# Finding where each node's run begins in a sorted edge list: marks multiplied with the list's differences instead of 49 gathers of rows

## The chip, the core and the metric

The kernel runs on one core of one Trainium2 chip. A core has a matrix engine (TensorE, PE in the profile), three elementwise engines (VectorE or DVE, ScalarE or ACT, GpSimd or POOL), a queue engine (SyncE, SP) and 16 DMA engines that all the queues share. Each engine works through its own list of instructions in order and waits for others by semaphores. The metric is the device time of one execution in microseconds. The kernel before takes 6495.99 us in the median of 5 runs (6495.36 to 6511.66).

## The reference, cut to what matters

The program is two layers of a graph network over 6250 nodes with 256 features. Each layer has a message-passing part, a linear attention part and a feed-forward part with experts. The last part of the second layer is a graph attention (GAT) that decides how the experts are weighted:

```python
src = jnp.concatenate([edge_index[0], loops])
dst = jnp.concatenate([edge_index[1], loops])
e = jax.nn.leaky_relu(a_src[src] + a_dst[dst], negative_slope=0.2)
e_max = jax.ops.segment_max(e, dst, num_segments=M)
ee = jnp.exp(e - e_max[dst])
denom = jax.ops.segment_sum(ee, dst, num_segments=M)
...
agg = jax.ops.segment_sum(msg, dst, num_segments=M)
```

The edge list has 131,072 random edges. The kernel sorts them by destination once. The sums and maxima over the edges of one node are then running scans over a stretch of the list, and for each node the kernel must know the place in the list where its stretch begins (`gfirst`) and where it ends (`glast`). The work in question computes those two tables of places.

## The kernel before, in words

**The sorted list.** `by_gat` is a table in DRAM of 128 runs of 1024 keys (128x1024 int32, 512 KB). A key holds the destination node in its upper bits and the source in its lower 13. Read row by row it is the list in order of the destination. It is finished long before it is used here.

**The places before (`gat_places`, line 701 on).** The place of node n is the number of keys smaller than n's least key. Nodes stand in 49 tiles of 128, one node a partition. First the 128 first keys of the runs are turned into a row by TensorE (lines 712 to 716), and for each of the 49 tiles one VectorE instruction counts how many of them are smaller (line 720): that gives the run that holds the node's first edge. Then, for each tile, an indirect DMA on POOL's queue fetches that run for each of the 128 nodes (the tile `grow`, 128x1024 f32, 512 KB; helper `gather`, line 770), and one VectorE instruction counts the smaller keys in it (line 734). The gather of tile t is issued two turns ahead of its count. The end of the function writes the places to DRAM and reads them back shifted by one node (lines 741 to 745), because the end of a stretch is the beginning of the next one.

**Where this runs.** `middle` (line 1535) sets up three pieces of work that share the engines. The main line is `experts` (line 1356): 32 slots of 512 rows, each slot with four column blocks, each block with two steps: the first products into a PSUM bank `ph` (line 1414) with a Gelu on ACT, and the second products of the slot before into `po` (line 1422) with a bias added by VectorE (line 1424). `turn` transposes the next slot's rows (line 1397). The weights and rows of a slot, 512 KB each, and its biases `mb` come over SP's queue. After the experts come `take_back`, which is 98 gathers, and `mix1`.

The second piece is `edge_sums`, which goes through 782 tiles of 128 edges: per tile one gather on POOL's queue (`ring<-in_edge_attr,edge_of`), one mark on VectorE (line 616), one product on TensorE (line 603), and per four tiles one addition on VectorE (line 594). It has 793 rounds; a gather is issued 11 rounds ahead of its product, into a ring of 15 buffers, so POOL can be at most a few rounds ahead of TensorE.

The third piece is `others`: `gat_places`, then `node_terms`, which fetches and adds rows per node with 98 gathers.

**What sets the order.** Everything is put into the queues in an order that is worked out when the program is built, from estimated costs. Each generator yields a cost for what it has just issued. `beside` lets `others` have 0.7 units for each unit of `edge_sums` (1.27 units a round); `step(3.8)` after each step of the experts lets that mixture issue 3.8 units, and `step(11)` does so 30 times in `mix1`. What is left when `mix1` is through is issued by `finish`. So a piece of `others` with smaller costs ends after fewer steps of the experts, and the rounds of `edge_sums` move with it. In this stretch there are 4 PSUM buffers named `mm`, given out in turn to `ph`, `po`, the transposes and everything else that asks for one, and 2 named `es` for the edge products.

Of the kernel before, what the change touches and what calls it, by code (L numbers as in the profile page):

```python
# [7 lines left out]
BF16 = mybir.dt.bfloat16  # L8
F32 = mybir.dt.float32
I32 = mybir.dt.int32  # L10
AF = mybir.ActivationFunctionType
OP = mybir.AluOpType
# [6 lines left out]
P = 128  # L19
N = 6250  # L20
NT = 49
# [6 lines left out]
W2C = E2 // P  # L28
# [8 lines left out]
NODE_BITS, NODE_ONE = 13, 1 << 26  # L37
# [20 lines left out]
NP_MASK = 8191  # L58


class Net:
# [639 lines left out]
    def gat_places(self, sp):  # L701

        nc = self.nc
        self.gfirst = self.const.tile([P, NT], I32, name="gfirst")
        self.glast = self.const.tile([P, NT], I32, name="glast")
        places = self.dram.tile([NP + 1, 1], F32, name="places")
        least = sp.tile([P, NT], F32, name="least")
        li = least.bitcast(I32)
        nc.gpsimd.iota(li, pattern=[[P, NT]], base=0, channel_multiplier=1)
        nc.vector.tensor_scalar(li, li, NODE_BITS, NODE_ONE, op0=OP.logical_shift_left, op1=OP.bitwise_or)  # L710
        heads = sp.tile([P, 1], F32, name="heads")
        nc.sync.dma_start(heads.bitcast(I32), self.by_gat[:, 0:1])
        ph = self.tr()
        nc.tensor.transpose(ph[:, 0:P], heads.to_broadcast([P, P]), self.ident)
        hrow = sp.tile([P, P], F32, name="hrow")
        nc.vector.tensor_copy(hrow, ph[:, 0:P])
        runs = sp.tile([P, NT], F32, name="gruns")
        junk = sp.tile([P, W2C], BF16, name="gjunk")
        for t in range(NT):
            nc.vector.tensor_scalar(junk[:, 0:P], hrow, least[:, t:t + 1], None, op0=OP.is_lt, op1=OP.add,  # L720
                                    accum_out=runs[:, t:t + 1])
            yield 0.4
        nc.vector.tensor_scalar(runs, runs, -1.0, 0.0, op0=OP.add, op1=OP.max)
        run = sp.tile([P, NT], I32, name="grun")
        nc.vector.tensor_copy(run, runs)
        inside = sp.tile([P, NT], F32, name="ginside")
        late = []
        for t in range(NT + 2):
            if t < NT:
                r = sp.tile([P, W2C], F32, name="grow", bufs=3)  # L730
                self.gather(r.bitcast(I32), self.by_gat, run[:, t:t + 1])
                late.append(r)
            if t >= 2:
                nc.vector.tensor_scalar(junk, late[t - 2], least[:, t - 2:t - 1], None, op0=OP.is_lt, op1=OP.add,
                                        accum_out=inside[:, t - 2:t - 1])
            yield 1.7
        first = runs
        nc.vector.scalar_tensor_tensor(first, runs, float(W2C), inside, op0=OP.mult, op1=OP.add)
        total = sp.tile([1, 1], F32, name="gtotal")
        nc.vector.memset(total, float(E2))  # L740
        nc.sync.dma_start(places[0:NP, :].rearrange("(t p) o -> p (t o)", p=P), first)
        nc.sync.dma_start(places[NP:NP + 1, :], total)
        end = sp.tile([P, NT], F32, name="gend")
        nc.sync.dma_start(end, places[1:NP + 1, :].rearrange("(t p) o -> p (t o)", p=P))

        none = inside
        nc.vector.tensor_tensor(none, first, end, op=OP.is_equal)
        past = sp.tile([P, 1], F32, name="gpast")
        nc.vector.tensor_scalar(past, self.lane, LAST - 0.5, None, op0=OP.is_gt)
        nc.vector.tensor_tensor(none[:, NT - 1:NT], none[:, NT - 1:NT], past, op=OP.max)  # L750
        nc.vector.tensor_scalar(none, none, float(OUT_OF_LIST), None, op0=OP.mult)
        nc.vector.tensor_add(self.gfirst, first, none)
        nc.vector.scalar_tensor_tensor(self.glast, end, -1.0, none, op0=OP.add, op1=OP.add)
        yield 1.0
# [1391 lines left out]
```

## Time and profile before

| what | value |
| --- | --- |
| median of 5 runs | 6495.99 us |
| the profiled execution: its own time, its span | 6506.26 us, 6504.4 us |
| mean granted TensorE clock | 0.730 |
| busy over the span: PE, DVE, ACT, POOL | 56%, 45%, 13%, 56% |
| `grow` gathers: 49, 947 ns median | 3094.4 to 3307.1 us (starts) |
| counts of line 734: 49, 1272 ns median | 3101.0 to 3319.1 us (starts) |
| `ring` gathers of `edge_sums`: 782 | 3027.8 to 4650.9 us (starts) |

Times in the trace are counted from the start of the span. "Busy" is the time in which an engine has an instruction at work, so a busy share far below one means waiting, and "idle before" names what ended the waiting. A float32 product of a 128x128 tile stands in the trace as two matmul records, one for each of its two passes. The granted clock is 1.0 or 0.5 at any moment; means over a stretch lie between.

### The profile page before, as it was taken

The numbers are of one execution on the slowest core, as the hardware profiler recorded it, in microseconds if no ns is written. First come the engines' busy times: TensorE is split into PE (matmuls) and PEld (weight loads), VectorE is DVE, ScalarE is ACT, GpSimd is POOL, SyncE is SP. The second block draws the span as 40 slices with busy tenths as digits, with TensorE's granted clock in tenths as the row PEclk, the third lists the DMA queues.
The fourth block names the chain that finished last, engine by engine and source line by source line (L and its number), as shares of the span: only waits on it lengthen the run. The fifth ranks groups of instructions, "written<-read, shape, count | busy, mean of one in ns | idle before, by whom it ended". The sixth has DMA issues, their size and how long they took to land. (4 is left out here: it accounts for less than half of the span.)

```text
span 6504.4 us, 55745 instructions
## 1 busy us (share of the span) xinstructions
PE 3630.3 (56%) x16292; PEld 2738.1 (42%) x16292; DVE 2898.2 (45%) x7864; ACT 871.3 (13%) x2058; POOL 3629.8 (56%) x4400
## 2 busy tenths in 40 slices
PE   5666655465656665364656677144653665555660
PEld 4555555445555554243434445033541333333340
DVE  5775555356666765563424443442420111111136
ACT  3650000040000000051111221010110111111120
POOL 1667777605656676225646566666457655555602
PEclk8787666687888867565878888567775776777675
DMA  5333323312222223123664443311231111111134
GB/s 182 91 110 102 88 85 87 94 55 84 86 84 84 86 86 88 49 71 118 210 132 142 134 137 119 86 50 47 73 90 15 34 40 33 36 37 36 37 102 148
DMA packets 382778, 563.72 MB, mean 87 GB/s; under 512 B 124687, under 2 KB 270278, under 8 KB 382286
## 3 DMA queue, kind: packets, MB, share of 16 engines
q0 software_dynamic: 150864, 331.19, 19.1%
q1 hardware_dynamic: 207812, 209.55, 10.3%
q10 hardware_dynamic: 23756, 18.97, 0.9%
q8 instruction: 143, 2.34, 0.1%
q14 instruction: 203, 1.66, 0.1%
HBM read 446.11 MB, written 113.72 MB: 86 GB/s over the span
## 5 line engine op out<-in xcount | busy, mean ns | idle before, releaser
L770 POOL DMA_INDIRECT ring<-table,src_of x1564 | 1597.9, 1022 | 1065.2 <-issue 333.6
L603 PE MATMUL es<-hot,ring 128*128 128x128 f32 x7820 | 1493.3, 347 | 1177.1 <-issue 476.4
L603 PEld LDWEIGHTS es<-hot,ring 128*128 128x128 f32 x7820 | 1314.8, 249 | 1419.4 <-issue 626.6
L770 POOL DMA_INDIRECT G<-gtab,glist x800 | 759.6, 949 | 440.4 <-DVE msg L1871 216.5
L770 POOL DMA_INDIRECT ring<-in_edge_attr,edge_of x782 | 746.2, 954 | 460.7 <-issue 183.1
L2064 PE MATMUL mm<-lw,lhT 128*128 128x256 f32 x1568 | 483.1, 428 | 534.9 <-issue 291.7
L618 DVE TENSOR_SCALAR hot<-numbers,node_of,w_of 128x128 f32<-128x128 f32 x1564 | 588.1, 402 | 217.4 <-remote 97.2
L2066 DVE TENSOR_TENSOR ly<-mm,lb 128x256 f32<-128x256 f32 x196 | 80.9, 422 | 1265.6 <-remote 773.9
L2064 PEld LDWEIGHTS mm<-lw,lhT 128*128 128x128 f32 x1568 | 326.5, 212 | 742.0 <-issue 453.1
L2056 PE MATMUL mm<-lxt,lw 128*128 128x512 f32 (+1 forms) x832 | 452.7, 663 | 64.8 <-issue 61.8
L1469 PE MATMUL mm<-ohot,ones 128*1 128x128 bf16 (+1 forms) x1564 | 152.3, 255 | 332.9 <-DVE ohot L1463 304.9
L594 DVE TENSOR_TENSOR BT<-BT,es 128x256 f32 x392 | 162.1, 414 | 375.8 <-remote 214.5
L1422 PE MATMUL mm<-mw,BT 128*128 128x256 f32 x1024 | 279.4, 419 | 63.1 <-DVE nv_node_vec_n L1498 27.5
L1414 PE MATMUL mm<-BT,mw 128*128 128x512 f32 x512 | 282.6, 677 | 55.5 <-issue 32.8
L2058 ACT ACTIVATE lhT<-mm,lb 128x512 f32<-128x512 f32 (+1 forms) x208 | 135.8, 663 | 1256.7 <-remote 876.1
L2056 PEld LDWEIGHTS mm<-lxt,lw 128*128 128x128 f32 x832 | 176.8, 219 | 234.4 <-issue 223.3
L1469 PEld LDWEIGHTS <-ones 128*1 128x1 bf16 (+1 forms) x1564 | 116.2, 105 | 365.8 <-issue 203.5
L616 DVE TENSOR_SCALAR hot<-numbers,from_of 128x128 f32<-128x128 f32 x782 | 241.0, 344 | 36.9 <-PE es L603 10.9
L1422 PEld LDWEIGHTS mm<-mw,BT 128*128 128x128 f32 x1024 | 208.4, 215 | 93.6 <-DVE nv_node_vec_n L1498 28.3
L1301 POOL DMA_INDIRECT chosen<-z,pos x98 | 99.3, 1013 | 262.7 <-DVE chosen L1224 206.1
L243 ACT COPY sx<-back 128x512 f32<-128x512 f32 x28 | 15.0, 589 | 1576.0 <-DMA ring<-table,src_of 979.4
L1474 DVE TENSOR_TENSOR deg<-deg,mm 1x128 f32 x392 | 108.8, 277 | 261.3 <-remote 102.4
(527 smaller groups left out, 4584.4 us busy)
## 6 DMA issues: line engine op xcount, KB each, us to landing
mw<-in_L_ffn_W SPq DMA_DIRECT2D x64, 512.0 KB
ring<-table,src_of POOLq DMA_INDIRECT x1564
ye<-ly SPq DMA_DIRECT2D x48, 512.0 KB
yes<-ye SPq DMA_DIRECT2D x48, 512.0 KB
xs<-chosen SPq DMA_DIRECT2D x32, 512.0 KB
yielded<-BT SPq DMA_DIRECT2D x32, 512.0 KB
G<-gtab,glist POOLq DMA_INDIRECT x800
ring<-in_edge_attr,edge_of POOLq DMA_INDIRECT x782
```

The lines of the kernel that those rows point to most:

```text
L594: nc.vector.tensor_tensor(dst, dst, ps[:, 0:h * P].rearrange("p (j n) -> p j n", j=h), op=OP.add)
L603: nc.tensor.matmul(ps[:, j * P:(j + 1) * P], lhsT=rows[:, j * P:(j + 1) * P], rhs=hot, start=(first and j == 0), stop=(last and j == h - 1))
L616: self.nc.vector.tensor_scalar(dst, self.numbers, node, None, op0=OP.is_equal)
L618: self.nc.vector.tensor_scalar(dst, self.numbers, node, w, op0=OP.is_equal, op1=OP.mult)
L770: self.nc.gpsimd.indirect_dma_start(out=dst, out_offset=None, in_=table, in_offset=bass.IndirectOffsetOnAxis(ap=idx, axis=0))
L1414: nc.tensor.matmul(ph, lhsT=w1s[s][:, j, c * P:(c + 1) * P], rhs=xTs[s % 2][:, j, :], start=(j == 0), stop=(j == 1))
L1422: nc.tensor.matmul(po[:, :C], lhsT=hTs[(s - 1) % 2][:, i, c * P:(c + 1) * P], rhs=w[:, i, :], start=(i == 0), stop=(i == 3))
L1469: nc.tensor.matmul(ps[0:row + 1, i // GE * P:(i // GE + 1) * P], lhsT=self.ones16[:, 0:row + 1], rhs=hot[:, i, :], start=(i % GE == 0), st ...
L1474: nc.vector.tensor_tensor(d, d, ps[row:row + 1, i * P:(i + 1) * P], op=OP.add)
L2056: nc.tensor.matmul(ph[:, :n * P], lhsT=w1[:, e, j, c * P:(c + 1) * P], rhs=xt[:, j, :n * P], start=(j == 0), stop=(j == 1))
L2058: nc.scalar.activation(hT[:, c, :n * P], ph[:, :n * P], AF.Gelu, bias=b1[:, e, c:c + 1])
L2064: nc.tensor.matmul(po[:, :C], lhsT=h0[:, i, c * P:(c + 1) * P], rhs=w2[:, e0, i, :], start=(i == 0), stop=(i == 3))
```

## The change

The places are computed without gathering runs. All of `by_gat` is brought on chip once as `node` (128x1024, one run a partition), and once more shifted down by one run as `prior`, whose first row is zero. The keys are cut to their destination node and turned into float32, and `node` becomes the difference between each run and the run before it. For a tile of nodes a matrix of marks is 1 where run r begins with a node smaller than the partition's node (run 0 always counts). The product of those marks with the differences adds up the differences of runs 0 to r, which is run r itself: TensorE so picks, for each node, the run that holds its first edge. It needs two products of 128x128 with 128x512 for the 1024 columns, and a third with a column of ones that counts the marks, which is the number of the run. VectorE counts the smaller nodes in the two halves straight from PSUM. The 49 gathers, the transposed heads and the 49 counts over the heads are gone. The end of the function (places to DRAM and back) stays. The costs that the function yields are 8, 3 and 2 units ahead of the loop and 0.2 and 1.4 a tile, where it was 0.4 and 1.7 a tile with two turns more.

```diff
-        least = sp.tile([P, NT], F32, name="least")
...
-        nc.sync.dma_start(heads.bitcast(I32), self.by_gat[:, 0:1])
-        ph = self.tr()
-        nc.tensor.transpose(ph[:, 0:P], heads.to_broadcast([P, P]), self.ident)
-        hrow = sp.tile([P, P], F32, name="hrow")
-        nc.vector.tensor_copy(hrow, ph[:, 0:P])
+        node = sp.tile([P, W2C], F32, name="gnode")
+        prior = sp.tile([P, W2C], F32, name="gprior")
+        nc.sync.dma_start(node.bitcast(I32), self.by_gat)
+        nc.vector.memset(prior[0:1, :], 0.0)
+        for a, n in ((0, 112), (112, 15)):
+            nc.sync.dma_start(prior.bitcast(I32)[a + 1:a + 1 + n, :], self.by_gat[a:a + n, :])
+        yield 8.0
+        for v in (node, prior):
+            vi = v.bitcast(I32)
+            nc.vector.tensor_scalar(vi, vi, NODE_BITS, NP_MASK, op0=OP.logical_shift_right, op1=OP.bitwise_and)
+            nc.vector.tensor_copy(v, vi)
+        nc.vector.memset(prior[0:1, :], 0.0)
+        yield 3.0
+        head = sp.tile([P, 1], F32, name="heads")
+        nc.vector.tensor_copy(head, node[:, 0:1])
+        nc.vector.memset(head[0:1, :], -1.0)
+        nc.vector.tensor_tensor(node, node, prior, op=OP.subtract)
+        ids = sp.tile([P, NT], F32, name="gids")
+        nc.vector.tensor_scalar(ids, self.iota[:, 0:NT], float(P), self.lane, op0=OP.mult, op1=OP.add)
         runs = sp.tile([P, NT], F32, name="gruns")
-        junk = sp.tile([P, W2C], BF16, name="gjunk")
+        inside = sp.tile([P, 2, NT], F32, name="ginside")
+        junk = sp.tile([P, 512], BF16, name="gjunk")
+        yield 2.0
         for t in range(NT):
-            nc.vector.tensor_scalar(junk[:, 0:P], hrow, least[:, t:t + 1], None, op0=OP.is_lt, op1=OP.add,
-                                    accum_out=runs[:, t:t + 1])
-            yield 0.4
+            hot = sp.tile([P, P], F32, name="gbelow", bufs=2)
+            nc.vector.tensor_scalar(hot, self.iota, float(t * P), head, op0=OP.add, op1=OP.is_gt)
+            yield 0.2
+            pr = [self.mm() for _ in range(2)]
+            for i in range(2):
+                nc.tensor.matmul(pr[i], lhsT=hot, rhs=node[:, i * 512:(i + 1) * 512], start=True, stop=True)
+            pc = self.mm()
+            nc.tensor.matmul(pc[:, 0:1], lhsT=hot, rhs=self.ones[:, 0:1], start=True, stop=True)
+            for i in range(2):
+                nc.vector.tensor_scalar(junk, pr[i], ids[:, t:t + 1], None, op0=OP.is_lt, op1=OP.add,
+                                        accum_out=inside[:, i, t:t + 1])
+            nc.vector.tensor_copy(runs[:, t:t + 1], pc[:, 0:1])
+            yield 1.4
         nc.vector.tensor_scalar(runs, runs, -1.0, 0.0, op0=OP.add, op1=OP.max)
-        for t in range(NT + 2):
-            if t < NT:
-                r = sp.tile([P, W2C], F32, name="grow", bufs=3)
-                self.gather(r.bitcast(I32), self.by_gat, run[:, t:t + 1])
-                late.append(r)
-            if t >= 2:
-                nc.vector.tensor_scalar(junk, late[t - 2], least[:, t - 2:t - 1], None, op0=OP.is_lt, op1=OP.add,
-                                        accum_out=inside[:, t - 2:t - 1])
-            yield 1.7
+        nc.vector.tensor_add(inside[:, 0, :], inside[:, 0, :], inside[:, 1, :])
+        inside = inside[:, 0, :]
```

More of the change, by code (lines that the diff above doesn't have):

```diff
@@ L706, in gat_places @@
         places = self.dram.tile([NP + 1, 1], F32, name="places")
-        least = sp.tile([P, NT], F32, name="least")
[L708 to L711, printed above, removed]
-        nc.sync.dma_start(heads.bitcast(I32), self.by_gat[:, 0:1])
-        ph = self.tr()
-        nc.tensor.transpose(ph[:, 0:P], heads.to_broadcast([P, P]), self.ident)
@@ L719, in gat_places @@
+        junk = sp.tile([P, 512], BF16, name="gjunk")
+        yield 2.0
         for t in range(NT):
-            nc.vector.tensor_scalar(junk[:, 0:P], hrow, least[:, t:t + 1], None, op0=OP.is_lt, op1=OP.add,
-                                    accum_out=runs[:, t:t + 1])
-            yield 0.4
-        nc.vector.tensor_scalar(runs, runs, -1.0, 0.0, op0=OP.add, op1=OP.max)
-        run = sp.tile([P, NT], I32, name="grun")
-        nc.vector.tensor_copy(run, runs)
-        inside = sp.tile([P, NT], F32, name="ginside")
@@ L727, in gat_places @@
-        late = []
-        for t in range(NT + 2):
-            if t < NT:
-                r = sp.tile([P, W2C], F32, name="grow", bufs=3)
-                self.gather(r.bitcast(I32), self.by_gat, run[:, t:t + 1])
-                late.append(r)
-            if t >= 2:
-                nc.vector.tensor_scalar(junk, late[t - 2], least[:, t - 2:t - 1], None, op0=OP.is_lt, op1=OP.add,
-                                        accum_out=inside[:, t - 2:t - 1])
-            yield 1.7
+            hot = sp.tile([P, P], F32, name="gbelow", bufs=2)
```

## The prediction

> **What bounds the stretch now.** I read first the table of windows over the stages in which the pieces share the engines. Its columns: stretch, length, busy time and count of PE, PE's weight loads, DVE, ACT and POOL, granted clock, DMA share, GB/s. The rows: the count of heads; the 49 gathers; the wait at the end of the places; `node_terms`; experts beside `edge_sums` alone; a stretch without such gathers.
>
> ```profile
> 3064.00:3093.00 29.00, 28.90 (x113) 18.88 (x114) 22.82 (x124) 11.23 (x15) 7.55 (x8) 0.90 0.37 114
> 3093.00:3322.00 229.00, 156.76 (x591) 109.56 (x590) 101.32 (x251) 29.05 (x42) 140.85 (x149) 0.81 0.62 209
> 3322.00:3354.00 32.00, 5.35 (x16) 2.70 (x15) 0.98 (x7) 0.00 (x0) 2.01 (x3) 0.66 0.83 8
> 3354.00:3971.00 617.00, 429.81 (x1700) 299.85 (x1700) 263.93 (x790) 119.17 (x220) 372.82 (x386) 0.87 0.46 139
> 3971.00:4077.00 106.00, 76.79 (x328) 58.10 (x328) 30.26 (x112) 11.27 (x15) 69.58 (x74) 0.82 0.29 81
> 4661.00:4757.00 96.00, 94.67 (x544) 85.23 (x544) 69.87 (x233) 39.47 (x81) 33.64 (x34) 0.96 0.39 124
> ```
>
> Count POOL's gathers: 149 in 229 us, 386 in 617, 74 in 106. That is one per 1.43 to 1.60 us whatever the mixture. So POOL's gathers set the pace there, though POOL is busy for only 0.60 to 0.66 of the time. The groups of the second row show what fills the pace:
>
> ```profile
> L770 POOL DMA_INDIRECT ring<-in_edge_attr,edge_of x100 | 94.6, 946 | 40.2 <-issue 26.6 <-remote 9.6 <-PE es L603 2.4
> L734 DVE TENSOR_SCALAR_CACHE_REDUCE gjunk<-grow,least 128x1024 bf16<-128x1024 f32 x49 | 62.4, 1273 | 16.1 <-DMA grow<-by_gat,grun 9.8 <-issue 6.0 <-DVE hot L616 0.2
> L770 POOL DMA_INDIRECT grow<-by_gat,grun x49 | 46.4, 946 | 51.1 <-DVE gjunk L734 34.5 <-issue 11.2 <-DVE grun L725 4.6
> ```
>
> A gather is 0.95 us and 0.30 us of issue: 1.25 us unhindered, 1.5 with the waits. Last, TensorE's order in time, for its prices:
>
> ```profile
> 3079.95 1.88 PE L1414 MATMUL mm<-BT,mw 128*128 128x512 f32 x4
> 3081.67 0.38 PE L603 MATMUL es<-hot,ring 128*128 128x128 f32 x2
> 3081.89 1.89 PE L1422 MATMUL mm<-mw,BT 128*128 128x256 f32 x8
> 3083.62 0.61 PE L603 MATMUL es<-hot,ring 128*128 128x128 f32 x4
> 3084.07 0.60 PE L1397 MATMUL mm<-ident,xs 128*128 128x128 f32 x4
> 3084.50 1.88 PE L1414 MATMUL mm<-BT,mw 128*128 128x512 f32 x4
> ```
>
> Differences of the starts, at the full clock: a step of the experts 1.72 us (so 0.43 for one pass over 512 columns), one round of edges 0.22, a transpose group 0.43.
>
> **What goes.** 49 `grow` gathers: 49 x 1.25 = 61 us of POOL, 74 at 1.5; 25.7 MB of the 47.95 MB that the DMA moved there. On DVE 49 x (1.273 + 0.083) = 66 us, and 49 counts of heads at 0.342 + 0.083 = 21 us. On PE the transposed heads; it waited for their load until 3064.09, though `xs` was issued five microseconds earlier (3054.42). I take 3 us for that; bounds are 0, if the weights are as late, and 5. A POOL iota of 0.19 us, a VectorE shift and two conversions of 0.2 go at no gain, beside idle time.
>
> **What comes, by engine.**
> DMA and SP: three loads of `by_gat`, 1 MB, in place of the one of the heads, issued at about 3059.5 behind the first slot's rows and weights and ahead of the second slot's. At the 209 GB/s of the row above 1 MB is 5 us. They land near 3069, and VectorE asks for them only after the fourth step, about then; if they are later, the edge marks and the additions of `po` stand behind that wait on VectorE, and TensorE behind those. The second slot's weights, issued at 3067, slip by up to 5 us; the 3 us from the heads cover them. The sum takes 0 for both together; the bounds are -5 and +5. The memset that the shifted load may wait for runs on an idle VectorE.
> DVE ahead of the loop: two shifts, two conversions, one subtraction of 128x1024. The rows at 128x800 are 0.572 us (shift), 0.570 (conversion) and 0.984 (two inputs), so about 0.72, 0.72 and 1.25 by length: 4.1 us once. DVE is idle for 128 of the 229 us.
> DVE a tile: the mark, between 0.22 (from 0.569 for 128x800 of plain one-input work) and 0.345 (line 616, from PSUM); two counts over 512 from PSUM, between 0.69 (a 128x512 copy from PSUM) and 1.27 (the whole 1024), I take 0.77 plus 0.083; a one-column copy, 0.15. Together some 2.2 us, against 1.36 + 0.43 before: 49 x 0.4 = 20 us more, in idle time as a sum; where it stands in the order is another matter (below).
> PE a tile: two products over 512 columns in two passes each, 4 x 0.43 = 1.72 us, and the counting product, two passes with the marks loaded again. No row has one column; with 24 columns (line 169, 160 records in 18.6 us) a pass is 0.116, so 0.23; bounds 0.05 and 0.8. Together 1.95 us, 49 x 1.95 = 96 us.
>
> **What moves.** The costs yielded fall from 107.3 to 92.4 units, and `edge_sums` gets 1/0.7 of that. Before, 107.3 + 107.3/0.7 = 261 units, less 6 of the first `step`, at 3.8 a step: 67 steps of the experts stand ahead of the end of the places; after, 92.4 + 132 = 224 units make 57. Followed through the loops, the first order has 20 transpose groups and 108 edge products there (the end comes behind the last `ph` of slot 8), the second 17 and 91 (behind the third `ph` of slot 7). `node_terms` and its rounds are unchanged behind it; ten steps move to where the experts run beside edges alone; 12 rounds of edges move out of `finish`.
>
> **The sum.** PE ahead of the end of the places, before: 67 x 1.72 + 20 x 0.43 + 108 x 0.22 = 148 us of the 258 between 3064 and 3322. After: 57 x 1.72 + 17 x 0.43 + 91 x 0.22 + 96 = 221 us. POOL has 91 x 1.25 to 1.5 = 114 to 137 us there, so TensorE becomes the bound. What can it do in practice? Where it was the bound beside edges (3064 to 3093: 12 steps, 6 groups, 12 products, 25.9 us) it took 29 us: 89%. So 248 us. To that come waits that the order makes. The mark of a tile is issued behind the addition of `po` on DVE in 27 of the 49 cases, and the tile's products follow directly. TensorE then waits for its own second products to be added (0.42), for two marks of edges (2 x 0.26) and for the tile's mark (0.22 to 0.345), less the edge products between: about 1.0 us, 27 us in all (bounds: 0, if the marks are early; 49 x 1.0). T = 275 us. The end of the places comes at 3061 + 275 = 3336 where it was 3322: +14. Its wait of 32 us for the places read back remains: VectorE stands, PE behind it, POOL behind PE, SP's next loads behind the readback. Then the ten steps that were not done: 106 us for 25 steps is 4.2 each, +42. At the end 12 rounds fewer: between 8 (20 us for 31 rounds from 4641 on) and 15 (12 x 1.25), I take -12, nearer the gathers since the last 11 rounds have none. The sum is +44, less 2 for transfers that no longer meet 512 KB gathers: **+42 us**. The profiled execution's 6506.3 becomes 6548; it lies 10 us above the median, so for the median 6496 + 42 = 6538 us.
>
> **Two rules of the Trainium skill.** The granted clock was 0.81 among the gathers and 0.90 where PE was dense beside edges. "TensorE: Matmul & The Clock Gate" (Part 1, The HAM clock gate) says that only an idle window of about 3.4 us halves the clock. By it waits of 1.0 us leave the clock alone and T stays 275; by the row of 0.81 T would be 334. Against the change speaks "SBUF — State Buffer" (the "DVE blocks DMA" trap): a VectorE instruction in a two-port mode, SBUF to SBUF, keeps POOL from writing the descriptors of its DMAs. The edge marks read PSUM, the new ones SBUF. By the rule POOL loses up to 49 x 0.345 = 17 us; by the rows POOL has over 100 us to spare there, and the sum stays.
>
> **The rivals.** With the other terms kept, the change is T - 233 us.
> *TensorE takes the places in its idle time* (faster). Place: the loop. For it: 110 us of PE's 258 are without work, and the halved DMA load could shorten the waits for weights. T = 221; 3 us more at the end (15 rounds' worth for 12), and the 10 us by which PE waits for `mb` behind the places, which 3 steps in place of 1 could cover: 221 - 233 - 3 - 10 = -25, 6471. Without those 13 us it is a clear gain only below T = 220. Against: no stretch beside edge gathers ran above 89%.
> *The change gives back what it takes* (no change). T between 220 and 246, the marks always early: 6483 to 6509. For it: 22 of the 49 marks stand behind a first product, whose 1.72 us hide them.
> *Buffers and clock* (much slower). Each tile takes three of the four `mm` buffers in turn, so the experts' next product waits for the tile's counts; gaps then keep the clock at 0.81: 221/0.81 = 273, over 0.89 = 307, + 27 = 334, so +101: 6597. For it: PE was held at 0.81 for 229 us. Against: there it waited for POOL, and longer products fill its gaps.
>
> **How the numbers follow.** A measurement here tells about 0.2%, 13 us. Chances: faster 0.12, no change 0.15, the sum (+13 to +70, 6509 to 6566) 0.50, much slower 0.23. So slower by over 0.2% has 0.73. Range 6487 to 6590, which cuts most of the faster case and the far end of the last.
>
> **What would show it.** Right: 49 x 6 new matmul records between 3080 and 3335 at 0.43 us a pass, PE over 85% busy there with POOL waiting for PE's `es`, the loop's waits on PE released by the new marks; the readback's wait at about 3336; the experts' end some 55 us later than 4077; a shorter stretch behind `mix1`. Wrong: PE under 75% busy with a buffer or VectorE as releaser and the clock near 0.8 (worse than the sum), the readback's wait ahead of 3295 (better), or a node load that lands after 3080 and holds VectorE.

## The result, and the profile after

The kernel after takes 6519.48 us in the median of 27 runs (6498.76 to 6536.15), beside 6499.58 us in 50 runs of the kernel before on the same chip: a ratio of 1.0031, 95% interval 1.0023 to 1.0038. It is slower by 20 us (15 to 25). 6538 was predicted, +42.

The experiments further down ran on three other chips. There the same kernel before takes 5441.4 to 5443.1 us, and the change costs more: 5486.9 against 5442.4 us, a ratio of 1.0085 (1.0068 to 1.0102), +44.5 us. That is within the 20 to 45 us expected before it ran there; the rival, that the 20 us of the first chip came from stalls that only that chip has, is out. The loop of the kernel before had been expected to take 250 to 270 us on any chip, since its waits are for its own gathers; it took 210 (below). So each experiment is compared by its ratio to the kernel before on its own chip, and its profile with profiles of the kernels before and after taken on such a chip.

The table of windows of the kernel after, on the first chip, for the stretches that answer those shown of before. The columns are the same: stretch, length, busy time and count of PE, weight loads, DVE, ACT and POOL, granted clock, DMA share, GB/s. The rows: the loop of the places; the wait at its end; `node_terms`; experts beside edges alone; the last edge rounds at the end of `finish`.

```profile
3071.00:3305.00 234.00, 214.03 (x831) 131.78 (x830) 126.75 (x434) 27.98 (x39) 84.63 (x90) 1.00 0.27 83
3305.00:3337.00 32.00, 8.65 (x36) 5.84 (x34) 1.27 (x11) 1.47 (x2) 1.54 (x2) 0.68 0.77 12
3337.00:3958.00 621.00, 438.11 (x1706) 305.69 (x1707) 267.41 (x803) 118.26 (x218) 374.75 (x388) 0.85 0.45 136
3958.00:4108.00 150.00, 102.02 (x441) 76.94 (x439) 38.13 (x140) 16.57 (x23) 96.21 (x102) 0.83 0.32 95
...
4665.00:4676.00 11.00, 6.80 (x38) 5.63 (x36) 4.05 (x13) 0.00 (x0) 0.00 (x0) 0.81 0.06 16
```

Read them against the rows of before. In the loop TensorE is busy for 214 of 234 us (before: 157 of 229) at a clock of 1.00 (0.81), POOL makes 90 gathers where it made 149, and the DMA moves 83 GB/s (209). The wait at the end of the places is 32 us as it was. `node_terms` took 617 us and takes 621. The stretch of edges alone took 106 us for 74 gathers and takes 150 for 102: +44. At the end, 20 us became 11.

The waits inside the loop, from the view of waits (engine and tile, released by; total us, times, longest):

```profile
POOL ring L785 <- PE es L603: 140.0, 63, 4.5
DVE gjunk L745 <- PE mm L741: 64.2, 44, 2.1
PE mm L741 <- DVE gbelow L737: 18.1, 23, 1.1
```

POOL and VectorE both wait for TensorE; TensorE waits for nothing much but the marks. The engine that ends last in this loop is now TensorE. The groups give the prices of the new instructions:

```profile
L741 PE MATMUL mm<-gnode,gbelow 128*128 128x512 f32 x196 | 94.7, 605 | 19.4 <-DVE gbelow L737 18.1 <-issue 0.7 <-DVE hot L616 0.6
...
L745 DVE TENSOR_SCALAR_CACHE_REDUCE gjunk<-mm,gids 128x512 bf16<-128x512 f32 x98 | 73.6, 751 | 75.9 <-PE mm L741 64.2 <-PE mm L1429 3.3 <-PE es L603 1.5
...
L737 DVE TENSOR_SCALAR gbelow<-iota,heads 128x128 f32<-128x128 f32 x49 | 14.8, 302 | 0.0
```

The passes start 0.43 us apart, the count takes 0.751 us (0.77 was estimated) and the mark 0.302 (between 0.22 and 0.345).

Along the chain of stages, after less before on the first chip: the places are written 15.5 us earlier (3305.6 against 3321.1). But 6.4 of these were there before the change begins to act, since the first load of the experts' rows is issued at 3048.0 and not at 3054.4. Counted from that load it is -9, where +14 was predicted. Then the readback -2, `node_terms` +4, edges alone +44, the taking back of the experts' rows -4, `mix1` with `finish` -12, of which the last edge rounds have -9, and what follows +3. By the profiles' spans the execution ends 18 us later, or 24 counted from that load. So two terms missed by some 24 us together on the way to the end of the places, and the rest came in within a few microseconds.

### The profile page after: what moved, and what is told of

It reads as the page before. It is cut to its first block, busy times and chain, and to the rows that moved or that the text cites. A ratio compares the mean times of both kernels' runs of the same rounds, so it can differ in the third digit from the quotient of the medians.

```text
span 6522.5 us, 56323 instructions
## 1 busy us (share of the span) xinstructions
PE 3701.8 (57%) x16585; PEld 2771.7 (42%) x16585; DVE 2917.9 (45%) x7970; ACT 872.5 (13%) x2058; POOL 3590.0 (55%) x4350
```

## The experiments

Two theories stood ahead of the experiments. Mine: the places cost what they cost TensorE, that is 96 us of products and 27 us of waits on marks, all on the path, against gathers that the loop had covered in part; and ten moved steps cost 4.2 us each. The main rival: the products are taken in idle time, and the loss comes from the moved rounds alone.

### One half of the products made twice

```diff
-            for i in range(2):
+            for i in (0, 0, 1):
                 nc.tensor.matmul(pr[i], lhsT=hot, rhs=node[:, i * 512:(i + 1) * 512], start=True, stop=True)
```

> The kernel after, with the first of the two 512-column products of each tile made twice into the same bank: 49 x 2 passes of 0.43 us, 42 us more of TensorE and nothing more for any other engine. Theory (TensorE bounds the loop of the places): the loop grows from 234 to 276 us and nothing takes it back, so 62 us over the kernel before (20 + 42), a ratio of 1.0095. Rival (VectorE's counts and marks, some 2.2 us a tile, hand out the pace): TensorE has room, at most 10 us more, 1.003 to 1.005.

Measured: 5528.75 us, ratio 1.0162 (1.0145 to 1.0179). Against the kernel after (1.0085) that is 0.0077 of 5442, or 42 us. The edit adds 49 products of two passes, 98 x 0.43 = 42 us. The window of the loop:

```profile
2676.00:2972.00 296.00, 275.35 (x984) 161.30 (x985) 133.36 (x449) 35.57 (x49) 86.77 (x92) 0.98 0.27 84
```

296 us, where the kernel after has 255 on such a chip (below). Every microsecond of product that is added in this place is paid in full. That the products are hidden there is ruled out.

### The change with the cost units of before

The yield at the end of a tile is raised so that the places hold the planner for as many units as before. Then the same number of expert steps and edge rounds stands ahead of their end as before, and nothing is moved.

```diff
-            yield 1.4
+            yield 1.704
```

> The kernel after with one yielded cost changed, 1.4 to 1.704 a tile, so that the function costs 107.3 units as before: 67 steps of the experts stand ahead of the end of the places again, and the last rounds of the edge pass are left for the end as before. Theory (the ten moved steps cost 42 us where they went, and 22 us where they were): the end of the places comes 22 us later, the stretch of experts beside edges alone is 44 us shorter, the end of the edge pass 9 us longer: 13 us less than after, some 7 us over before, 1.001. Rival (the same work in another order takes the same time): 1.003.

Measured: 5490.63 us, ratio 1.0092 (1.0075 to 1.0109): 4 us above the kernel after, with intervals that overlap, as the rival had it. For comparison the kernel after on such a chip, its rows for the loop, the write of the places, their readback, edges alone, and `mix1` with `finish`:

```profile
2671.00:2926.00 255.00, 233.04 (x885) 142.61 (x886) 133.45 (x449) 35.57 (x49) 86.83 (x92) 0.98 0.32 97
2926.00:2951.00 25.00, 7.97 (x32) 5.25 (x31) 0.00 (x0) 1.46 (x2) 0.94 (x1) 0.73 0.90 6
2951.00:2957.00 6.00, 0.00 (x0) 0.00 (x0) 0.26 (x2) 0.00 (x0) 0.00 (x0) 0.50 0.64 24
...
3467.00:3589.00 122.00, 102.07 (x440) 73.98 (x440) 41.20 (x152) 16.83 (x23) 92.13 (x99) 0.92 0.40 119
...
3756.00:4098.00 342.00, 225.69 (x857) 165.70 (x857) 128.44 (x435) 32.40 (x68) 246.18 (x260) 0.73 0.21 51
```

and this kernel's loop, edges alone, and `mix1` with `finish`:

```profile
2679.00:2950.00 271.00, 251.33 (x981) 156.89 (x982) 141.42 (x475) 40.67 (x56) 102.15 (x108) 0.99 0.34 104
3494.00:3578.50 84.50, 70.36 (x323) 51.68 (x324) 29.84 (x111) 11.27 (x15) 63.76 (x69) 0.98 0.33 95
3745.50:4102.50 357.00, 238.62 (x881) 173.94 (x881) 133.34 (x451) 32.43 (x68) 258.61 (x272) 0.71 0.20 52
```

The stretch of edges alone is 37.5 us shorter, as the term for the ten steps has it. But the loop is 16 us longer and the end 15 us longer. The steps and rounds that were moved are work that has to be done somewhere: 16 + 15 us here, or 37.5 us there. From the first load of the experts' rows to the end the two profiles differ by 0.4 us. As a cause of the loss, the moving falls: it is an exchange, nearly at par.

### The kernel before without its gathers of runs

```diff
-                r = sp.tile([P, W2C], F32, name="grow", bufs=3)
-                self.gather(r.bitcast(I32), self.by_gat, run[:, t:t + 1])
+                if t == 0:
+                    r = sp.tile([P, W2C], F32, name="grow")
+                    nc.vector.memset(r, 0.0)
```

> The kernel before without its 49 gathers of runs: the counts read one tile of zeros, so the places, and what the attention reads by them, are left out of the computation. Theory (each gather on POOL's queue costs about 1.5 us of the pace of its stretch): the stretch of 229 us has 100 gathers in place of 149 and takes about 150 us, near TensorE's own 137; 75 us less than before, 0.9885. Rival (the counts of 1.27 us on VectorE or the transfers of the weights hold the stretch): 20 to 40 us less, 0.994 to 0.997.

This kernel leaves the places out. Measured: 5373.0 us, ratio 0.9873 (0.9856 to 0.989), 68 us under the kernel before, as the theory had it. Its loop, and then the loop and edges alone of the kernel before on such a chip:

```profile
2688.00:2838.00 150.00, 149.99 (x688) 108.22 (x687) 124.28 (x374) 39.89 (x56) 101.48 (x108) 0.99 0.54 170
```

```profile
2681.00:2891.00 210.00, 164.38 (x694) 115.37 (x693) 125.49 (x375) 40.06 (x57) 144.33 (x153) 0.90 0.71 243
...
3436.00:3522.00 86.00, 70.33 (x322) 52.06 (x322) 30.14 (x111) 11.26 (x15) 64.97 (x70) 0.97 0.33 95
```

Without the gathers TensorE is busy for 149.99 of 150 us. The prediction had counted 148 us of TensorE's work there, and nothing stands between it and that number: TensorE beside edges reaches not 89% but all of the time. The gathers add 60 us to that loop. The other 8 us are in the attention, far behind it: from its first load to the end it takes 1395 us in the kernel before and 1387 us here. Why is open; here the attention also reads by places that were not computed.

This run and the one above have the same plan, so their difference, 0.0219 of 5441 us or 119 us, is the price of the places by products, less the some 6 us by which this kernel alone still waits for the heads (below). That makes 125 us, against 96 + 28 by the products (counted) and the marks' waits (measured below): two ways that agree. By gathers the places cost 68 us. What is left, 119 - 68 = 51 us, is the loss of the run above (50 us) by construction and no third check.

### The marks a tile ahead

```diff
+        hots = {}
+        def mark_of(t):
+            if t < NT:
+                hots[t] = sp.tile([P, P], F32, name="gbelow", bufs=3)
+                nc.vector.tensor_scalar(hots[t], self.iota, float(t * P), head, op0=OP.add, op1=OP.is_gt)
+        mark_of(0)
         for t in range(NT):
-            hot = sp.tile([P, P], F32, name="gbelow", bufs=2)
-            nc.vector.tensor_scalar(hot, self.iota, float(t * P), head, op0=OP.add, op1=OP.is_gt)
+            mark_of(t + 1)
+            hot = hots.pop(t)
```

> After, with the mark of a tile made a tile ahead of its products (three buffers for it in place of two), so that no product waits on its mark. Theory (the 18 us that the products waited on marks in the profile of after are on the path): 12 to 18 us under the kernel after. Rival (edge products fill TensorE in the meantime, or TensorE is bound by the reads of the two counts on VectorE): within 4 us of the kernel after. The wait of the products on the mark goes to under 3 us by either.

Measured: 5459.35 us, ratio 1.0036 (1.0023 to 1.0048), 27 us under the kernel after: more than was expected. The loop in its window, and the group of the products:

```profile
2675.50:2902.50 227.00, 225.22 (x885) 141.67 (x886) 132.98 (x449) 35.57 (x49) 86.76 (x92) 0.99 0.35 109
...
L747 PE MATMUL mm<-gnode,gbelow 128*128 128x512 f32 x196 | 92.3, 593 | 0.6 <-DVE gbelow L739 0.6
```

The same two views of the kernel after on such a chip had 255 us and this group, with its weight loads:

```profile
L741 PE MATMUL mm<-gnode,gbelow 128*128 128x512 f32 x196 | 94.7, 606 | 19.4 <-DVE gbelow L737 19.4
...
L741 PEld LDWEIGHTS mm<-gnode,gbelow 128*128 128x128 f32 x196 | 34.1, 190 | 53.4 <-issue 27.8 <-DVE gbelow L737 25.2 <-DVE hot L616 0.2
```

The wait for the marks goes from 19.4 us to 0.6, and the loop shrinks by 28. The row of the matmuls understates the wait, since the marks are the weights and their load (25.2 us of waiting, 27 times in the view of waits) stands ahead of the matmul's own record. What is left, 227 us with TensorE busy for 225, is the prediction's 221 us of work and 6 more.

### Edge rounds between the write of the places and their use

```diff
         nc.sync.dma_start(places[NP:NP + 1, :], total)
+        yield 14.0
         end = sp.tile([P, NT], F32, name="gend")
         nc.sync.dma_start(end, places[1:NP + 1, :].rearrange("(t p) o -> p (t o)", p=P))
+        yield 6.0
```

> After, with edge rounds put between the write of the places and the load that reads them back (14 us of TensorE's work by the planner's prices) and between that load and its use (6 us). Theory (VectorE stands for the 32 us of write, readback and their use, and every mark of an edge round is queued behind it, so TensorE stands too): the stretch of 32 us with TensorE busy for under 7 of it is gone, and the kernel is 18 to 28 us faster than the kernel after. Rival (the rounds put there are taken from the stretch of node terms, whose own waits on gathers then come earlier): TensorE's stand goes and the time stays within 8 us of the kernel after.

Measured: 5476.43 us, ratio 1.0058 (1.0037 to 1.0079): 10 us under the kernel after by the medians, 15 by the ratios, between the two expectations. The write of the places, edges alone, and `mix1` with `finish`:

```profile
2932.00:2961.00 29.00, 14.04 (x68) 10.23 (x66) 5.91 (x21) 1.47 (x2) 7.55 (x8) 0.82 1.30 40
...
3492.00:3563.00 71.00, 60.64 (x277) 44.18 (x275) 26.57 (x97) 9.70 (x13) 53.63 (x58) 0.98 0.36 103
...
3729.00:4091.00 362.00, 238.17 (x889) 173.47 (x889) 135.25 (x456) 32.38 (x68) 261.57 (x276) 0.72 0.21 52
```

Up to the last row taken back the kernel is 33 us faster, counted from TensorE's first turn of rows in both. Then it loses 20: `mix1` with `finish` takes 362 us in place of 342, with 276 gathers in place of 260. The 20 units that were yielded counted against the budget that the experts' steps hand out, though nothing was issued for them, so rounds of edges stayed over for `finish` (the next run tests this). My rival had them taken from `node_terms`; they were taken from the end.

### Marks ahead, end spread, and the units given back

Both edits together, and the last yield of the places changed so that the units paid come back:

```diff
-        yield 1.0
+        yield -19.0
```

> After, with the marks a tile ahead and edge rounds between the write of the places, its readback and its use, but the 20 us of rounds that are put there are given back to the plan after, so that no rounds fall to the finish. Theory (both stands, 27 us of waits on marks and 33 us at the readback, are TensorE's own, and the run with the end spread lost 20 of its 33 to rounds that the plan held for done and the finish had to make): 45 to 60 us under the kernel after, that is 0 to 15 us under the kernel before, with the finish as long as in the kernel after (342 us from the last row taken back to the attention). Rival (the stretch of node terms is bound by its gathers, and what the end of places gives is lost there): 27 to 35 us under the kernel after, 10 to 18 over the kernel before.

Measured: 5432.48 us, ratio 0.9982 (0.9973 to 0.9992). That is 56 us under the kernel after by the ratios, and 10 under the kernel before, as the theory had it. The loop, the write of the places, edges alone, and `mix1` with `finish`:

```profile
2675.00:2902.00 227.00, 224.97 (x882) 141.22 (x883) 132.34 (x445) 35.59 (x49) 86.13 (x92) 0.98 0.35 109
2902.00:2933.00 31.00, 14.86 (x72) 10.95 (x70) 6.50 (x26) 1.47 (x2) 9.81 (x11) 0.81 1.22 57
3414.00:3536.00 122.00, 100.97 (x440) 73.29 (x440) 41.31 (x152) 16.73 (x23) 92.13 (x99) 0.93 0.40 119
3702.00:4043.00 341.00, 224.40 (x857) 164.94 (x857) 129.35 (x436) 32.39 (x68) 246.50 (x261) 0.74 0.20 52
```

`mix1` with `finish` is back at 341 us. Beside the run with the marks alone it is 29 us faster (1.0036 to 0.9982), so of the 56 us 27 go with the marks and 29 with the readback; no run has the readback with its units given back alone. By the profiles the 29 us lie between the write of the places and the end of `node_terms`: 512 us here (2902 to 3414), 541 in the kernel after (2926 to 3467). The kernel before has the same stand of 31 us, so the mend should be open to it too, but no run tried that.

### The heads of before loaded earlier than used

```diff
         nc.sync.dma_start(heads.bitcast(I32), self.by_gat[:, 0:1])
+        yield 6.0
         ph = self.tr()
```

> Before, with edge rounds between the load of the 128 marks' heads and the product that uses them. Theory (the kernel before waits at its start some 6 us longer on the heads than on the experts' rows, and the change took that wait away): TensorE's first turn of rows starts 3.5 us after their load is issued and not 9.5, and the stretch to the end of places is 3 to 8 us shorter. Rival (the rows come late too and the heads hide behind them): it starts at over 8 us after. In the time neither can be told from no change: ratio 0.998 to 1.001.

Measured: 5433.09 us, ratio 0.9981 (0.9972 to 0.999), 10 us under the kernel before, at the lower edge of what was expected. TensorE's first turn of rows starts 3.6 us after the load of the rows is issued (2682.3 against 2678.7); in the kernel before it is 9.4 us (2680.9 against 2671.5), on the first chip 9.7. So the heads cost 6 us, and the change saves them. The stretch to the end of the places is not 3 to 8 us shorter, as expected, but longer (229 us from that load, before 219), because the 6 units put more work ahead of it: 743 matmuls where there were 694. The other 4 us are not explained.

### The places beside the sublayer after the experts

`node_terms` goes first, and the places are made one piece to each edge round from round 884 of the plan on, which is in `mix1`. Their units are not counted. Between the write of the places, their readback and its use 25 and 8 edge rounds are put.

```diff
+    def spread_out(self, work, other, first):
+        for i, cost in enumerate(work):
+            yield cost
+            if i >= first:
+                next(other, None)
+        for _ in other:
+            pass
...
-                self.after_this(self.beside(self.edge_sums(edge), others(), 0.7))
+                both = self.beside(self.edge_sums(edge), self.alone(self.node_terms), 0.7)
+                self.after_this(self.spread_out(both, self.alone(self.gat_places), 884))
```

> The kernel after with the places taken out of the experts: node_terms goes first beside the edge pass, and the places follow one piece per round of the edge pass from about the start of mix1, without a cost of their own; between the write of the places, the read and its use lie 25 and 8 rounds, so that nobody stands 32 us for it. Theory (places cost where TensorE is the bound, and are free where POOL is): mix1 has 388 us in which TensorE is at work for 175 and POOL sets the pace; it stays near 388, the 234 us of the loop go, and the experts beside edges alone take their steps at 4.2 us: 49 gathers at 1.5 and the wait of 32 us gone against before, 70 to 110 us less, 0.983 to 0.989. Rival (the work only moves): mix1 grows by 96 us of TensorE or 108 of VectorE, and the whole is no faster than before, 1.00 or above.

Measured: 5433.94 us, ratio 0.9989 (0.9979 to 0.9999): 52 us under the kernel after, but only 7 under the kernel before, far from what I expected. A window from the middle of the places, `mix1` with `finish`, and two waits from 3750 to 3891 us:

```profile
3750.00:3800.00 50.00, 41.63 (x168) 24.31 (x167) 37.02 (x125) 4.98 (x9) 24.73 (x27) 1.00 0.14 35
...
3685.00:4039.00 354.00, 254.40 (x1007) 168.09 (x1007) 196.75 (x657) 31.54 (x68) 178.11 (x188) 0.86 0.23 37
...
POOL ring L798 <- PE es L612: 58.2, 38, 2.8
...
PE mm L750 <- DVE gbelow L746: 23.6, 31, 0.8
```

One tile for two edge rounds takes 3.38 us. TensorE is busy for 83% of the time at full clock and stands for marks; POOL makes 27 gathers in 50 us, where beside `mix1` alone it makes 41. So TensorE and the marks it stands for set the pace in this place as well, and no longer POOL. The experts end as early as in the kernel before (3519 and 3522 us) and leave 188 gathers for this part where that left 272, but it takes 354 us, where 357 were needed for the 272: what was gained was spent here.

### The places where TensorE has nothing to do

In the stretch that takes the experts' rows back, TensorE has no instruction at all. The kernel before on such a chip, that stretch and then `mix1` with `finish`:

```profile
3555.00:3689.00 134.00, 0.00 (x0) 0.00 (x0) 74.30 (x191) 0.00 (x0) 101.41 (x108) 0.50 0.34 99
3689.00:4046.00 357.00, 237.53 (x881) 172.64 (x881) 133.08 (x450) 32.30 (x68) 257.61 (x272) 0.71 0.20 51
```

The version above is changed so that `take_back` asks for half a tile in each of its 52 rounds, and the rest is asked for in every third edge round. The marks are a tile ahead, and 8 and 3 pieces stand about the readback in place of 25 and 8.

```diff
-            if i >= first:
+            if i >= first and (i - first) % 3 == 0:
                 next(other, None)
...
+            next(self.places_work)
             self.step(20.0)
+            next(self.places_work)
+            next(self.places_work)
             for i in range(NT + 3):
+                next(self.places_work)
```

> The places' products taken out of the experts' stretch again, as in the run that put them beside the sublayer after it, with the marks a tile ahead, but 26 tiles are made in the stretch that takes the experts' rows back, half a tile to each round of it, and the other 23 beside the sublayer after, one tile to six edge rounds. On a chip where the kernel before takes about 5441 us: TensorE had no instruction at all in the 134 us of the taking back, and VectorE 75 us of work; 26 tiles add 26 x 2.1 = 55 us to VectorE, so that stretch stays under 145 us. In the sublayer after, TensorE was busy for 240 of 357 us; 23 tiles of 2.3 us fit. Theory (a tile costs its time only where TensorE is the engine that ends last): the price of the places falls from the 68 us that the gathers cost before to 10 to 25: 40 to 60 us under the kernel before, ratio 0.989 to 0.993. Rival (the stretch after is then late by its own chain of matmuls and reads, as it was with the tiles there one to a pair of rounds): within 20 us of the kernel before, with the sublayer after and the finish at over 380 us together.

Measured: 5370.71 us, ratio 0.9861 (0.9845 to 0.9876), 76 us under the kernel before by the ratio and 122 under the kernel after. It beats both, and by more than the 40 to 60 us expected. The rows of edges alone, of the taking back, of `mix1` with `finish`, and of two windows in it:

```profile
3188.00:3531.00 343.00, 276.23 (x1206) 197.47 (x1206) 109.62 (x404) 47.05 (x65) 259.18 (x276) 0.95 0.42 125
...
3564.00:3697.00 133.00, 94.23 (x149) 37.09 (x147) 110.38 (x333) 0.00 (x0) 100.77 (x106) 0.62 0.35 100
3697.00:3984.00 287.00, 201.49 (x851) 140.75 (x851) 145.83 (x498) 31.78 (x68) 178.53 (x188) 0.83 0.31 45
...
3800.00:3850.00 50.00, 38.84 (x163) 24.47 (x161) 30.53 (x106) 5.28 (x11) 37.81 (x41) 0.93 0.21 53
...
3866.00:3893.00 27.00, 3.41 (x12) 2.57 (x13) 2.46 (x11) 0.00 (x0) 8.98 (x10) 0.52 1.35 25
```

The taking back lasts 133 us as before, with 94 us of products in it at a mean clock of 0.62: slow products, but nobody waits for them. `mix1` with `finish` takes 287 us, where the version with all tiles there took 354 for the same 188 gathers. In the first of the two windows POOL makes 41 gathers in 50 us, as many as beside `mix1` alone. So in both places the gathers keep their pace, and the products cost them nothing that can be measured.

The rest of the work is not free. The second window is the readback: POOL makes 10 gathers in 27 us, and TensorE waits 25 us for gathered rows (3860 to 3900). And behind the last gather this part goes on for 24 us (3959.7 to 3983.7), where the kernel before has 8 (4038.4 to 4046.3): there the sublayer's own work ends last, and no longer the gathers. The whole takes the time of the kernel that makes no gathers of runs (0.9873), but that one waits for the heads as well and has another plan, so their equality does not price the places. How much of the step from the version with all tiles in `mix1` is due to the marks ahead and how much to the place, no run separates.

## Why the prediction came out as it did

Right were the direction, a time within the range, and the mechanism: TensorE becomes the bound and pays for the products. The size was 42 us where the first chip measured 20. Going through the steps:

- **TensorE becomes the bound, and its work is 221 us.** Right. The passes start 0.43 us apart; the loop with the marks ahead takes 227 us with TensorE busy for 225; 98 added passes cost 42 us.
- **"What can it do in practice? ... 89%. So 248 us."** This is the step that failed. It turned one stretch of 29 us, which started with TensorE's clock not yet granted in full (0.90 over the stretch), into a rate for 250 us. In the loop itself the clock was 1.00, and TensorE did 148 us of counted work in 150 (gathers left out) and 221 in 227 (marks ahead). In those 29 us TensorE was busy for 28.9: 25.9 us of work at a clock of 0.90 are 28.8, so the whole loss of that stretch is the clock at its start. The term was some 6 us at the start, not 27.
- **27 us of waits on marks.** Right, 28 by the run that took them away. The profile's own row for it (18.1 us on the first chip) is too small, because the weight loads wait first. So T, the time from TensorE's first turn of rows to the end of the places, was 221 + 28 + 6 = 255 us, not 275: 254 us on the first chip, from the first turn at 3051.6 to the end of the places at 3305.6, and 255 on the other.
- **The heads, 3 us with bounds 0 and 5.** Mis-sized: 6 us on the first chip (3.6 us after the load of the rows, 9.7 before), outside the bounds. The node loads did not come late; nothing was lost by them.
- **The wait of 32 us at the readback remains.** Right, on both kinds of chips. That some 29 us of it can be had by order alone, the prediction did not see.
- **Ten moved steps, +42, and 12 rounds fewer at the end, -12.** Right as rows: +44 and -9 on the first chip, +36 and -15 on the other. But they are no price of the change. With nothing moved the kernel costs the same within 4 us, since the rounds are then in the loop and at the end.
- **The rivals.** TensorE did not take the places in idle time in this loop; elsewhere it does, which the last experiment shows. Buffers and a clock of 0.81 did not come: 23 waits of up to 1.1 us left the clock at 1.00, and with the gathers left out the loop of before ran at 0.99, so its 0.81 went with the waits for gathers. That agrees with "TensorE: Matmul & The Clock Gate" (Part 1, The HAM clock gate), by which it takes an idle window of about 3.4 us to halve the clock. The readback, with TensorE almost without work for over 20 us, is where the clock fell, to 0.73 and then 0.50.
- **"SBUF — State Buffer" and its "DVE blocks DMA" trap.** The gathers took 947 ns each in the loop after, 946 before, and no wait of POOL on the marks stands among its largest. No loss is seen here; no run tried the rule by itself.

On the first chip the predicted +42, with 21 us less in T and 3 more saved at the heads, makes +18, where +20 was measured. On the other chips T is the same, but the loop of before takes 210 us there and not 257: 47 us more. Against that, edges alone grow by 36 and not 44, the end shrinks by 15 and not 9, and the attention's part is 8 us shorter (1387 us against 1395 from its first load to the end). That makes 18 + 47 - 8 - 6 - 8 = +43, where +44.5 was measured. Near the predicted number it lands there by chance: the gathers were cheaper to keep, and the products cheaper to make, than the prediction had it. The 8 us in the attention were not followed up; the two profiles on such chips that have the gathers of runs show 1395 us there, those without them 1387 to 1391.

## What to carry to other kernels

Work that is moved to another engine costs nothing only where something else sets the pace and goes on setting it; look in the table of windows for a stretch in which that engine has little or nothing to do, and put it there, since in a stretch where that engine ends last every microsecond is paid. Before an efficiency below one goes into a sum, look whether it is a rate or a fixed loss at the start of the stretch. And when a planner works with costs, units that are yielded for waiting must be given back, and rounds that are moved are an exchange, which a sum may not book as a loss by itself.

## What was not expected of the hardware

The same program takes 6500 us on one chip and 5441 to 5443 us on three others. The loop of before takes 257 us on the one and 210 on the others; the loop of after, which TensorE bounds, takes 254 and 255. On the first chip's profile of the kernel after, 11.8% of the chain that ended last is put down to "another core or an unknown queue"; on the other chip no such share is listed and the attention's gathers, POOL `G`, stand first with 14%. Why the one chip is slower was not settled. A gain or loss measured on one chip is, for work that gathers, not that of another: here it was 20 us and 44.5 us for the same change.
